# Sending token rows to expert slots: pacing each send by an earlier send's arrival instead of by a step's work

## The chip, the cores and the metric

The kernel runs on one core of a Trainium2 chip. A core has five engines that work side by side and wait for each other by semaphores: PE (TensorE, matrix products), DVE (VectorE), ACT (ScalarE), POOL (GpSimd) and SP (SyncE, which here only issues DMAs). DMAs run on 16 engines that all issuers share. The metric is the device time in microseconds; each figure is the median of several runs of the same program.

## The reference: what is computed

One transformer block over 8 sequences of 512 tokens of width 128. The rows are normalized. One branch is causal attention with 16 heads of width 8. The other is a mixture of experts: a shared feed-forward network for all tokens, and 8 expert networks of which each token uses the best two. Both read the same normalized rows, and their sum is added to the input.

```python
x = L0_attn_x
xn = _layernorm(x, axis=-1)
x = x + _L0_attn_ref(xn, ...) + _L0_ffn_ref(xn, ...)

# in _L0_ffn_ref
shared = _ffn(xf, shared_gate, shared_up, shared_down)
probs = jax.nn.softmax(xf @ gate_w.T, axis=-1)
topw, topi = jax.lax.top_k(probs, TOP_K)
...
acc + _ffn(xf, gw, uw, dw) * wcol[:, None]     # for each expert
```

with `_ffn` = `silu(x @ gw.T) * (x @ uw.T) @ dw.T`. There are 4096 tokens, hence 8192 pairs of a token and one of its experts.

## The kernel before

Attention runs in 160 steps: 32 groups of four heads (8 sequences with four groups each), five tiles of scores a group. A step fills a tile of scores on PE (`fill`, L322), takes its exponential on ACT (`weigh`, L446, line L450), and works seven tiles ahead on the rows' maxima (`look`, L810; PE L372, DVE L401 and L407). A step later the exponentials are multiplied with the values (`attend`, L464, line L473). From step 40 on (`BUSY`, L51) the causal mask of the diagonal tiles is no longer added by PE (L333) but cut out by POOL with a select (L458), queued behind the last send.

The feed-forward work is spread between the attention's steps, as a stream of pieces (`experts`, L718): 14 pieces of shared work (`EARLY`), then 36 pieces of routed work (two blocks of 128 slots each), then the rest of the shared work. A piece has three chunks (`chunk`, L663: four or eight products into gu, a tanh at L679, two DVE instructions at L680 and L681) and a product down (`down`, L694).

Routed work takes its rows from a table in HBM, `slots`, in which each expert has a run of blocks. `clear` (L871) first fills it with empty rows. `route` (L976), spread over the steps from the first one on, computes for each token its two experts and the two slots; the slots stand in SBUF (`slot`, L1055). Then each of the 32 rows of 128 tokens is sent twice, 64 indirect DMAs of 128 rows of 130 numbers (520 bytes), issued by POOL (`send`, L750, line L752). `load_slots` (L625) reads a block pair back into `s` after all 64 sends, the first three from POOL and the later ones from SP (L633), and `turn_slots` (L640) transposes it on PE (L648).

The order of PE, DVE, ACT and SP is the order in which the program writes their instructions. POOL's order is made by the tile framework from the dependencies and the program's order; every engine executes its own instructions in order, so one that waits holds up all behind it. In the sixth step (step 5) `route` puts the 64 sends on a list, and from then on each step takes two of them from it: one (L1248) gets a dependency on that step's exponential (`last_exp`), the other (L1259) on the last product of the step's gating (`last_gate`, L681), or on the exponential where the step has no gating. Two in a step make 32 steps, 5 to 36. Behind the sends POOL has the three loads of `s`, the selects from step 40 on, and later the returns of the routed results (L685).

Of the kernel before, what the change touches and what calls it, by code (L numbers as in the profile page):

```python
# [11 lines left out]
F32 = mybir.dt.float32  # L12
I32 = mybir.dt.int32
BF16 = mybir.dt.bfloat16
AF = mybir.ActivationFunctionType
ALU = mybir.AluOpType
# [7 lines left out]
SYNC = mybir.DependencyInfo(mybir.DependencyClass.Sync, mybir.DependencyReason.DATA)  # L24

P = 128
B, S, E = 8, 512, 128
H, D = 16, 8
NC = S // P
NT = B * NC  # L30
# [12 lines left out]
TOPK = 2  # L43
# [7 lines left out]
BUSY = 40  # L51
WIPED = 12
AT_ONCE = 2
EXPERTS_AT = 10
WEIGHTS_AT = 70
ROW = E + 2
# [9 lines left out]
def attn_moe_kernel(  # L66
# [15 lines left out]
    nc = tc.nc  # L82
    const = ctx.enter_context(tc.tile_pool(name="const", bufs=1))
# [45 lines left out]
    for i in range(NV):  # L129
        t = const.tile([P, NC, H, 32], F32, name=f"v_ext{i}")  # L130
# [65 lines left out]
    rows_attT = const.tile([P, NT, ROW], F32, name="rows_attT")  # L196
# [5 lines left out]
    for i in range(2 * TOPK):  # L202
        t = const.tile([P, NT], F32, name=f"best{i}")
        best.append(t)
    weight = const.tile([P, TOPK, NT], F32, name="weight")
    slot = const.tile([P, TOPK, NT], I32, name="slot")
# [3 lines left out]
    slots = dram1.tile([NB * BLK, ROW], F32, name="slots")  # L210
# [3 lines left out]
    def pool(name, bufs, **kw):  # L214
        return ctx.enter_context(tc.tile_pool(name=name, bufs=bufs, **kw))
# [3 lines left out]
    at = pool("at", 2)  # L219
# [102 lines left out]
    def fill(n, kind, j, bare):  # L322

        ps = w_ps.tile([P, 2, S], F32, name="scT")

        def part(out_, jj, width):
            q, k = rows_of(n, jj)
            i = NC - width // P
            nc.tensor.matmul(  # L329
                out_, lhsT=k[: QK + 3, ts(i, P)], rhs=q[: QK + 3, i * P :], start=True, stop=bare  # L330
            )
            if not bare:
                nc.tensor.matmul(out_[:, :P], lhsT=ident16, rhs=mask_k, start=False, stop=True)  # L333

        for t in range(2):
            if kind == "half":
                for u in range(2):
                    part(ps[:, t, ts(u, 2 * P)], 2 * t + u, 2 * P)
                continue
            at_ = 0  # L340
            for w in (S,) if kind == "wide" else (3 * P, P):
                part(ps[:, t, at_ : at_ + w], j + t, w)
                at_ += w
        return ps
# [96 lines left out]
                mT[ts(r, 16)],  # L441
            )

    last_exp, last_gate = [], []

    def weigh(n, kind, j, on_pool):  # L446

        ps = fill(n, kind, j, on_pool)
        pT = pr.tile([P, 2, S], F32, name="pT")
        last_exp[:] = [nc.scalar.activation(pT, ps, AF.Exp, scale=D**-0.5).ins]  # L450
        if on_pool:
            if kind == "half":
                diagonals = [pT.rearrange("p t (u k) -> p (t u) k", u=2)[:, :, :P]]
            else:
                diagonals = [pT[:, :, :P]] + ([pT[:, :, 3 * P :]] if kind == "mixed" else [])
            with tc.issue_after(sent[-1]):
                for d in diagonals:
                    nc.gpsimd.affine_select(  # L458
                        out=d, in_=d, pattern=[[0, d.shape[1]], [1, P]], compare_op=ALU.is_ge,
                        fill=0.0, base=0, channel_multiplier=-1,  # L460
                    )
        return pT
# [148 lines left out]
    later_pools = {}  # L611
    for_routed = ExitStack()
    sent, returned, stored = [], [], []

    def load_weights(k, c):

# [46 lines left out]
    def chunk(k, f):  # L663

        w, sT = turned[k]
        if f == 0:
            h_new = hid.tile([P, NF, PAIR], F32, name="h")
            hidden[k] = h_new
        h = hidden[k]
        gu = gu_ps.tile([P, 2, PAIR], F32, tag="gu", name="gu")  # L670
        for i in range(2):
            for c in range(len(w)):
                part = ts(c, PAIR // len(w))
                nc.tensor.matmul(  # L674
                    gu[:, i, part], lhsT=w[c][:, ds(i * FP + f * P, P)], rhs=sT[:, part],
                    start=True, stop=True,
                )
        th = res.tile([P, PAIR], F32, name="th")
        nc.scalar.activation(th, gu[:, 0], AF.Tanh, scale=0.5)  # L679
        nc.vector.scalar_tensor_tensor(th, th, 1.0, gu[:, 0], ALU.add, ALU.mult)  # L680
        last_gate[:] = [nc.vector.tensor_tensor(h[:, f], gu[:, 1], th, ALU.mult).ins]  # L681

    def give_back(k, c, o):

# [55 lines left out]
            load_weights(k + 2, 1)  # L740
        yield None, [partial(down, len(stream) - 1, c) for c in range(MB)]

    to_send = []

    def send_one(behind):

        if to_send:
            send(*to_send.pop(0), behind)

    def send(i, t, behind):  # L750

        d = nc.gpsimd.indirect_dma_start(  # L752
            slots, bass.IndirectOffsetOnAxis(ap=slot[:, i, t : t + 1], axis=0),
            rows_attT[:, t, :], None,
        )
        tc.add_manual_dep(d.ins, behind.name, SYNC, reason="in their step")
        if sent:
            tc.declare_no_dep(d.ins, group="sends", reason="no two pairs share a slot")
        tc.add_to_no_dep_group("sends", d.ins)
        sent.append(d.ins)  # L760
# [80 lines left out]
    def begin(step):  # L841
        for f in first.pop(step, []):
            more = f()
            if more is not None:
                more()
# [130 lines left out]
    def route():  # L976
# [73 lines left out]
        for i in range(TOPK):  # L1050
# [2 lines left out]
            own_sum = ro.tile([P, NT], F32, name=f"own_sum{i}")  # L1053
            nc.vector.tensor_reduce(own_sum, own, AX.X, ALU.add)
            nc.vector.tensor_copy(slot[:, i], own_sum)  # L1055
        to_send.extend((i, t) for t in range(NT) for i in range(TOPK))
        for _ in range(EXPERTS_AT):
            yield

# [93 lines left out]
    for b in range(5, B):  # L1153
        norm_rows(b)
    clear(0, AT_ONCE, unit_there)

# [25 lines left out]
    for t in range(FIRST):  # L1182
        step = t - FIRST
        begin(step)
        if t == NTILES:

            def onward():
                shift(0, parts_then)()
                clear(AT_ONCE, NB // WIPED, fetch(1))

# [32 lines left out]
    for n in range(B * NG):  # L1223
        b, g = divmod(n, NG)
        waiting = []
        for i, (kind, j) in enumerate(TILES):
            step = n * NTILES + i
            begin(step)
            if step in fetches:
                fetch(fetches[step])  # L1230
            on_pool = BUSY <= step < total_steps - 3
            waiting.append((kind, j, weigh(n, kind, j, on_pool)))

            if step - 1 in MORE:
                some_chunks(step, False)
                parts_then = look(step)
            else:
                parts_then = look(step)
                some_chunks(step, False)
            if step in light:  # L1240
                warm(5)
            parts_then()
            if step not in MORE and len(looked) < total_steps:
                prepare(*divmod(len(looked), NTILES))
            some_routing()
            if step >= WEIGHTS_AT:
                next(weighing, None)
            send_one(last_exp[0])  # L1248
            for f in late:
                f()  # L1250
            late = []
            if i == 1 and n % 2 == 0:
                av = av_ps.tile([P, S], F32, name="av")
            if i in (1, 3, 4):
                late = [partial(attend, n, waiting, av)]
                waiting = []
            side(step, 2)
            some_chunks(step, True)
            send_one((last_gate or last_exp)[0])  # L1259
            last_gate.clear()  # L1260
            if step in MORE:
                look(step)()
            if len(stored) == NB // MB:
                if not all_back:
                    for_routed.close()
                    later_pools["got"] = pool("got", 6)
                all_back.append(step)
            for _ in range(2 if len(all_back) > 1 else 0):
                if to_collect:
                    at_b = to_collect.pop(0)  # L1270
                    collect(at_b)
                    at_ = min(all_back[0] + 3 + 4 * at_b // 5, total_steps - 1)
                    due(at_, partial(weigh_second, at_b))
                    due(at_, partial(add_up, at_b, 0))
                    due(min(at_ + 1, total_steps - 1), partial(add_up, at_b, 1))

                    if (at_b + 1) * NC <= MB * EARLY and at_ + 2 < total_steps:
                        due(max(at_ + 2, last_shift), partial(store, at_b))
                    elif at_b < B - 1:
                        due(total_steps, partial(store, at_b))  # L1280
        if n == B * NG - 1:
            continue
        if n % 2:
            late.append(partial(evacuate, n, av))
            due(step + 2, partial(divide, n))
        if g == NG - 1:
            due(step + 3, partial(turn, b))
            due(step + 4, partial(join, b))
# [80 lines left out]
```

## Time and profile before

| | us |
|---|---|
| median of 3 runs (589.58 to 595.20) | 593.87 |
| the profiled execution's own time | 604.34 |
| its span | 602.6 |
| busy PE / DVE / ACT / POOL | 565.3 / 456.8 / 376.9 / 235.7 |
| sends on POOL: 64, first and last start | 67.6 and 187.3 |
| first PE instruction that reads `s` | 202.5 |

The profile shows one execution, with times from the start of its span. A group's line gives the source line, engine, operation, what is written and read, how often, and then the busy time, the mean of one in ns, the idle time of the engine just before these instructions and what ended most of it. A timeline's row gives start and length in us, and in brackets the idle time before it and its releaser. A send's length on POOL is the time of its issue; its bytes move later, and its arrival is told by a semaphore that gets sixteen steps.

### The profile page before, as it was taken

The numbers are of one execution on the slowest core, as the hardware profiler recorded it, in microseconds if no ns is written. First come the engines' busy times: TensorE is split into PE (matmuls) and PEld (weight loads), VectorE is DVE, ScalarE is ACT, GpSimd is POOL, SyncE is SP. The second block draws the span as 40 slices with busy tenths as digits, with TensorE's granted clock in tenths as the row PEclk, the third lists the DMA queues.
The fourth block names the chain that finished last, engine by engine and source line by source line (L and its number), as shares of the span: only waits on it lengthen the run. The fifth ranks groups of instructions, "written<-read, shape, count | busy, mean of one in ns | idle before, by whom it ended". The sixth has DMA issues, their size and how long they took to land.

```text
span 602.6 us, 13692 instructions
## 1 busy us (share of the span) xinstructions
PE 565.3 (94%) x4814; PEld 412.1 (68%) x4814; DVE 456.8 (76%) x1194; ACT 376.9 (63%) x698; POOL 235.7 (39%) x362
## 2 busy tenths in 40 slices
PE   6988899899988999999999999999999999999986
PEld 4756476567665677767777678777677777777643
DVE  6678958777765888777788687887687778787566
ACT  5624554564544767676667767686567767676574
POOL 9521345544554133334343334433434233433420
PEclk9888899999998999999999999999999999999987
DMA  7735244143144484839676585849666585843085
GB/s 215 240 71 225 77 127 112 41 124 90 45 112 129 131 230 133 250 101 265 208 175 206 168 226 177 207 156 217 194 198 212 173 211 198 218 136 109 4 265 154
DMA packets 52380, 98.39 MB, mean 163 GB/s; under 512 B 10070, under 2 KB 35546, under 8 KB 50152
## 3 DMA queue, kind: packets, MB, share of 16 engines
q1 hardware_dynamic: 45960, 83.65, 49.1%
q0 software_dynamic: 5360, 13.66, 6.7%
q8 instruction: 38, 0.62, 0.5%
q10 hardware_dynamic: 992, 0.21, 0.2%
q14 instruction: 30, 0.25, 0.1%
HBM read 73.36 MB, written 24.26 MB: 162 GB/s over the span
## 4 chain that ended last, share of the span: by engine, by line
PE 75%; ACT 9%; DVE 6%; DMA 4%; issue 3%; POOL 2%; SPq 1%; ACTq 0%; DVEq 0%; POOLq 0%
PE gu L674 21%; PE av L473 12%; PE y L701 11%; PE scT L329 10%; PE sc_diag L372 5%; PE sc_left L372 5%; ACT pT L450 2%; ACT sc_diag L360 2%; DMA qs<-dq 2%; DVE peaks L401 2%; PE qk_ps L246 2%; ACT th L679 1%; PE s_ps L648 1%; PE scT L333 1%; DMA w<-in_w_exp_dram 1%
## 5 line engine op out<-in xcount | busy, mean ns | idle before, releaser
L450 ACT ACTIVATE pT<-scT 128x1024 f32<-128x1024 f32 x160 | 164.0, 1025 | 66.6 <-PE scT L333 20.6
L685 POOL DMA_INDIRECT results<-o,goes x72 | 73.2, 1017 | 129.5 <-ACT o L707 118.6
L674 PE MATMUL gu<-sT,w 128*128 128x128 f32 x864 | 116.4, 277 | 1.7 <-DMA w<-in_w_exp_dram 1.1
L458 POOL TENSOR_SCALAR_AFFINE_SELECT pT<-pT 128x256 f32<-128x256 f32 (+1 forms) x163 | 70.3, 448 | 117.6 <-ACT pT L450 114.7
L401 DVE TENSOR_REDUCE peaks<-sc_diag 128x4 f32<-128x512 f32 x128 | 88.0, 687 | 33.5 <-PE sc_diag L372 22.5
L674 PEld LDWEIGHTS gu<-sT,w 128*128 128x128 f32 x864 | 108.1, 191 | 6.6 <-PE sc_diag L372 2.2
L329 PE MATMUL scT<-qs,ks 75*128 75x384 bf16 (+3 forms) x512 | 104.3, 304 | 5.1 <-ACT pT L450 5.0
L680 DVE SCALAR_TENSOR_TENSOR th<-th,gu 128x256 f32<-128x256 f32 x156 | 65.2, 418 | 38.5 <-ACT th L679 35.4
L679 ACT ACTIVATE th<-gu 128x256 f32<-128x256 f32 x156 | 59.7, 383 | 54.8 <-PE gu L674 31.5
L473 PE MATMUL av<-pT,v_ext 128*32 128x512 f32 (+3 forms) x1024 | 92.0, 455 | 0.0
L752 POOL DMA_INDIRECT slots<-rows_attT,slot x64 | 61.7, 964 | 76.1 <-ACT th L679 18.3
L372 PEld LDWEIGHTS <-qs 72*128 72x128 bf16 x896 | 65.1, 98 | 36.5 <-issue 18.0
L401 DVE TENSOR_REDUCE peaks<-sc_left 128x4 f32<-128x512 f32 x128 | 87.1, 680 | 0.0
L360 ACT CAST sc_diag<-mask_q 128x512 f32<-128x512 bf16 x115 | 68.1, 592 | 19.0 <-DVE peaks L401 10.0
L372 PE MATMUL sc_diag<-ks,qs 72*128 72x128 bf16 (+1 forms) x576 | 62.2, 225 | 8.9 <-ACT sc_diag L360 8.3
L681 DVE TENSOR_TENSOR h<-gu,th 128x256 f32<-128x256 f32 x156 | 66.2, 424 | 5.4
L701 PEld LDWEIGHTS y<-w,h 128*128 128x128 f32 x432 | 54.4, 191 | 22.3 <-issue 10.4
L701 PE MATMUL y<-w,h 128*128 128x128 f32 x432 | 64.1, 285 | 1.3 <-ACT v_ext L296 1.3
L372 PE MATMUL sc_left<-ks,qs 72*128 72x128 bf16 (+1 forms) x320 | 61.9, 275 | 3.3 <-DVE peaks L401 3.3
L329 PEld LDWEIGHTS <-ks 75*128 75x128 bf16 x512 | 47.0, 99 | 21.3 <-issue 10.2
L674 PE MATMUL gu<-xnT,ws_sb 128*128 128x256 f32 x192 | 53.0, 399 | 1.1 <-DVE h L681 0.9
L473 PEld LDWEIGHTS av<-pT,v_ext 128*32 128x32 f32 x1024 | 23.8, 110 | 31.1 <-issue 22.1
(185 smaller groups left out, 635.2 us busy)
## 6 DMA issues: line engine op xcount, KB each, us to landing
w<-in_w_exp_dram SPq DMA_DIRECT2D x72, 576.0 KB
qs<-dq SPq DMA_DIRECT2D x45, 192.0 KB
ks<-dk SPq DMA_DIRECT2D x45, 192.0 KB
slots<-empty POOLq DMA_DIRECT2D x6, 780.0 KB
s<-slots SPq DMA_DIRECT2D x33, 130.0 KB
r<-results SPq DMA_DIRECT2D x16, 256.0 KB
dq<-parts SPq DMA_DIRECT2D x7, 384.0 KB
dk<-parts SPq DMA_DIRECT2D x7, 384.0 KB
```

The lines of the kernel that those rows point to most:

```text
L329: nc.tensor.matmul(out_, lhsT=k[: QK + 3, ts(i, P)], rhs=q[: QK + 3, i * P :], start=True, stop=bare)
L360: nc.scalar.copy(diag_ps.rearrange("p (b k) -> p b k", k=P), mask_q.unsqueeze(1).to_broadcast([P, NC, P]),)
L372: nc.tensor.matmul(out_, lhsT=q[:QK, ts(c, P)], rhs=k[:QK, keys], start=start, stop=stop, skip_group_check=True,)
L401: nc.vector.tensor_reduce(peaks[:, i, 8 + 4 * t : 12 + 4 * t], banks[t].rearrange("p (b k) -> p b k", k=P), AX.X, ALU.max,)
L450: last_exp[:] = [nc.scalar.activation(pT, ps, AF.Exp, scale=D**-0.5).ins]
L458: nc.gpsimd.affine_select(out=d, in_=d, pattern=[[0, d.shape[1]], [1, P]], compare_op=ALU.is_ge, fill=0.0, base=0, channel_multiplier=-1,)
L473: nc.tensor.matmul(av[32 * jj : 32 * jj + 32, c * P :], lhsT=v_ext[b % NV][:, c, 4 * g + jj, :], rhs=weights, start=(n % 2 == 0 and c == 0 ...
L674: nc.tensor.matmul(gu[:, i, part], lhsT=w[c][:, ds(i * FP + f * P, P)], rhs=sT[:, part], start=True, stop=True,)
L679: nc.scalar.activation(th, gu[:, 0], AF.Tanh, scale=0.5)
L681: last_gate[:] = [nc.vector.tensor_tensor(h[:, f], gu[:, 1], th, ALU.mult).ins]
L685: d = nc.gpsimd.indirect_dma_start(results, bass.IndirectOffsetOnAxis(ap=goes_of[k][:, c : c + 1], axis=0), o, None, bounds_check=NP - 1, ...
L701: nc.tensor.matmul(y, lhsT=h[:, f, ts(c, P)], rhs=w[c % len(w)][:, ds(2 * FP + f * P, P)], start=(f == 0), stop=(f == NF - 1),)
```

## The change

The list of sends, the two calls in a step, and the notes of the last exponential and gating go. All 64 sends are written down at once where the list was made. From the third on, each has a memset of a scratch tile (128 x 384 numbers) on POOL ahead of it, and that memset waits for the arrival of the send two places in front; the send is queued behind its memset. The order of the sends stays the same.

```diff
+UNDER_WAY = 2
...
-    last_exp, last_gate = [], []
...
-        last_exp[:] = [nc.scalar.activation(pT, ps, AF.Exp, scale=D**-0.5).ins]
+        nc.scalar.activation(pT, ps, AF.Exp, scale=D**-0.5)
...
+    ticks = const.tile([P, 384], F32, name="ticks")
...
-        last_gate[:] = [nc.vector.tensor_tensor(h[:, f], gu[:, 1], th, ALU.mult).ins]
+        nc.vector.tensor_tensor(h[:, f], gu[:, 1], th, ALU.mult)
...
-    to_send = []
-
-    def send_one(behind):
-
-        if to_send:
-            send(*to_send.pop(0), behind)
-
-    def send(i, t, behind):
-
-        d = nc.gpsimd.indirect_dma_start(
-            slots, bass.IndirectOffsetOnAxis(ap=slot[:, i, t : t + 1], axis=0),
-            rows_attT[:, t, :], None,
-        )
-        tc.add_manual_dep(d.ins, behind.name, SYNC, reason="in their step")
+    def send(i, t):
+
+        with ExitStack() as order:
+            if len(sent) >= UNDER_WAY:
+                tick = nc.gpsimd.memset(ticks, 0.0)
+                tc.add_manual_dep(
+                    tick.ins, sent[-UNDER_WAY].name, SYNC, reason="few under way at a time"
+                )
+                order.enter_context(tc.issue_after(tick.ins))
+            d = nc.gpsimd.indirect_dma_start(
+                slots, bass.IndirectOffsetOnAxis(ap=slot[:, i, t : t + 1], axis=0),
+                rows_attT[:, t, :], None,
+            )
...
-        to_send.extend((i, t) for t in range(NT) for i in range(TOPK))
+        for t in range(NT):
+            for i in range(TOPK):
+                send(i, t)
...
-            send_one(last_exp[0])
...
-            send_one((last_gate or last_exp)[0])
-            last_gate.clear()
```

## The prediction

> **What bounds the kernel now.** I read the page first: busy time, then the chain of waits, then the costliest groups.
>
> ```profile
> PE 565.3 (94%) x4814; PEld 412.1 (68%) x4814; DVE 456.8 (76%) x1194; ACT 376.9 (63%) x698; POOL 235.7 (39%) x362
> PE 75%; ACT 9%; DVE 6%; DMA 4%; issue 3%; POOL 2%; SPq 1%; ACTq 0%; DVEq 0%; POOLq 0%
> L752 POOL DMA_INDIRECT slots<-rows_attT,slot x64 | 61.7, 964 | 76.1 <-ACT th L679 18.3
> ```
>
> PE is the bound and makes 75% of the chain; POOL has 2% of it. The third line is the 64 sends that the change re-orders: 0.964 us each on POOL. The releasers in front of them (view of waits, POOL, 67 to 205 us):
>
> ```profile
> POOL slots L752 <- ACT th L679: 18.3, 9, 2.5
> POOL slots L752 <- ACT pT L450: 14.3, 7, 3.7
> POOL slots L752 <- issue: 11.8, 30, 0.9
> POOL slots L752 <- DVE h L681: 7.6, 10, 2.0
> ```
>
> So POOL, not PE, waits for the steps: 61.7 us of sends and 58.8 us of idle time (76.1 less the 17.3 ahead of the first) make the stretch from 67.63 to 188.21 us. The question is therefore not what the sends cost but who waits for the last of them. The timeline of POOL at that place:
>
> ```profile
> 182.31 0.96 POOL L752 DMA_INDIRECT slots<-rows_attT,slot  x1 [0.31 <-DVE h L681]
> 183.58 0.96 POOL L752 DMA_INDIRECT slots<-rows_attT,slot  x1 [0.30 <-issue]
> 187.25 0.96 POOL L752 DMA_INDIRECT slots<-rows_attT,slot  x1 [2.71 <-DVE x_sb L711]
> 191.87 2.27 POOL L633 DMA_DIRECT2D s<-slots  x3 [3.66 <-DMA slots<-rows_attT,slot]
> 201.17 0.41 POOL L458 TENSOR_SCALAR_AFFINE_SELECT pT<-pT 128x256 f32<-128x256 f32 x1 [7.03 <-ACT pT L450]
> 204.55 0.41 POOL L458 TENSOR_SCALAR_AFFINE_SELECT pT<-pT 128x256 f32<-128x256 f32 x1 [2.97 <-ACT pT L450]
> ```
>
> The last send starts at 187.25 and lands at 191.1 by its semaphore. Three loads of s follow (free at 194.14), then POOL is idle for 7.03 us. The first s lands at 194.45, 2.6 us after its issue; PE reads it first at 202.5 (LDWEIGHTS s_ps). That is 8.0 us of slack for s, 7.0 us for the first select. Where the wire is busy (windows):
>
> ```profile
> 78.70:87.50 8.80, 8.52 (x79) 6.02 (x77) 5.79 (x12) 5.24 (x9) 4.06 (x5) 1.00 0.64 166
> 97.20:105.00 7.80, 7.20 (x67) 4.87 (x66) 6.19 (x15) 3.88 (x6) 4.51 (x5) 1.00 0.71 177
> 124.00:143.00 19.00, 18.37 (x161) 13.54 (x159) 14.75 (x35) 11.13 (x19) 9.40 (x10) 1.00 0.54 151
> 164.30:172.50 8.20, 7.36 (x61) 5.34 (x60) 6.15 (x15) 4.32 (x7) 4.47 (x6) 1.00 0.71 166
> 184.90:191.90 7.00, 5.30 (x29) 2.67 (x29) 3.35 (x8) 2.20 (x4) 0.99 (x2) 0.76 0.62 189
> ```
>
> The columns are length, busy PE, PEld, DVE, ACT, POOL, clock, DMA share, GB/s. Outside these five stretches the DMA share from 87 to 185 us is 0.12 to 0.19. In them q, k (or the first w) are moved by SP's queue, and a send lands late.
>
> **The change, part by part.**
>
> *Waits removed.* 60 waits of POOL for a step's exp or gating go. ACT and DVE did nothing for them, so nothing is saved there: 0.
>
> *Fills added.* 62 memsets of 128x384. POOL's memsets of 128x128 take 0.20 us and of 128x1560 1.39 us (groups by form), so 0.83 ns an element and 0.20 + 256 x 0.00083 = 0.41 us. 62 x 0.41 = 25.4 us of POOL, which had 58.8 us idle in this stretch.
>
> *Pitch where the wire is quiet.* In the trace a send lands (last of its sixteen semaphore steps) 2.27 us after its start: those started at 119.16, 121.15 and 125.67 took 2.27, 2.27 and 2.32. Send, fill, send: 0.96 + 0.41 + the 0.30 us that stand ahead of every send even when it waits for nothing ("issue" above) = 1.67 us. The send one place ahead started 1.67 us earlier, so at the next fill it is 1.67 + 0.96 = 2.63 us old and has landed. POOL, not the wait, sets the pace. Bounds: without the 0.30 us, 1.37 (then the wait sets (2.27 + 0.41 + 0.05)/2 = 1.37 as well). A select that follows a return mostly starts with no gap, but 12 of 72 show 0.25 to 0.27 us; if every fill pays that, 1.94. I take 1.67, as 41 of the 72 have no gap at all.
>
> *Pitch in the five bursts.* Sends started there landed after 6.5, 6.3, 5.0, 3.7 (first burst), 4.2, 6.2 (second), 6.2, 7.2, 4.3 (third), 5.0, 7.6, 3.5 (fourth), about 5.5 us; here the new wait binds. Two per 5.5 + 0.08 + 0.41 + 0.30 = 6.3 us is 3.1 us each. The bursts last 8.8 + 7.8 + 12 (from 131 to 143) + 8.2 + 5.5 = 42 us and hold 13.5 sends.
>
> *End of the stream.* Start 67.63, 1.3 for the second send, 42 in bursts, (62 - 13.5) x 1.67 = 81.0: the last send starts near 191.9 and lands at 194.2, 3 us later than before. s is issued then at 194.9 and lands at 197.5, 5.0 us before PE needs it. POOL is free at 197.2, 4 us before the exp of the first select ends. The cost is 0; what hides it is those 5 and 4 us. Without that cover each 0.1 us of pitch costs 6.3 us.
>
> *Rule against row.* The Trainium skill, "DMA: Bandwidth & Descriptors", section "Anatomy of one DMA — SWDGE (gpsimd) path", fits a DMA from this queue as 2.0 us plus bytes / 436e3. A send is 128 x 520 bytes, so an estimate of 2.15 us at all times. With it the wait never binds and the last send lands at 67.6 + 1.3 + 62 x 1.67 + 2.15 = 174.6. The quiet rows agree (2.27), the bursts (3.5 to 7.6) do not; I take the rows, 194.2. PE needs neither before 202.5.
>
> *Who queues behind a waiting fill.* On POOL: the other sends, the three s loads, the selects from step 40 on, later the returns. For them wait PE (s_ps, av) and, in SP's queue, the s loads from 208.27 on, which wait for all sends. Before step 40 nothing else is on POOL.
>
> *POOL's writes beside DVE.* No fill lies beside DVE work in the trace. The nearest row is the select: `second` (DVE, two operands in SBUF) has a median of 151 ns and up to 601, and the eight that meet a select average 0.25 us more. Small DVE instructions of that kind in the stretch: 7 each of L416, L421 to L424, 3 of L255, 4 of L261, 42. Fills cover 25.4 of 124 us; with the instruction's own length about a quarter are met: 42 x 0.25 x 0.25 = 2.6 us at most. The skill's "SBUF — State Buffer", section "SBUF: two separate sides", speaks against filling from GpSimd at all (it shares a port pair with VectorE, and one blocks the other for a whole instruction), but limits it for two-operand instructions to GpSimd work that reads SBUF; a memset only writes, so 0. Below nothing is excluded: a fill frees nobody. These instructions work some tiles ahead of their use and DVE is idle a quarter of the stretch; DVE has 6% of the chain, so 0.06 x 2.6, rounded to 0.2 us.
>
> *SP and the wire.* The same bytes move. At most two sends are under way instead of up to four in a burst, so q and k land sooner if anything. No PE, ACT or DVE wait from 60 to 215 us ends with a DMA: 0. PE's whole idle time in the five stretches is 0.3 + 0.6 + 0.6 + 0.8 + 1.7 = 4.0 us; that bounds a gain.
>
> *Sum.* 0 + 0 + 0.2 us, against the profiled execution's 604.34 us (602.6 of span and 1.7 around it). That run is 1.8% above the median of 593.87; a change of 0.2 us carries over as it is: 594.1 us.
>
> **Rivals.**
>
> *The stream comes late (slower).* If each fill pays the 0.27 us gap, the quiet pitch is 1.94: 67.6 + 1.3 + 42 + 48.5 x 1.94 = 205.0, landing 207.3, s there at 210.6, 8 us after PE asks for it. PE's order is fixed, so it stands: 602 us. If besides every send in a burst takes the worst 7.6 us (8.4 per two, 10 sends), 52 x 1.94 + 42 + 68.9 = 211.8, s at 217.5: +15 us, 609. It decides once the last send lands past 199.1 (202.5 - 2.6 - 0.8). For it: only 5 us of cover, 62 fills in one chain. Against: gapless starts are the common case.
>
> *Less crowding (faster).* If PE's idle time in the bursts comes from transfers, up to 4.0 us go: 590. Against it: no such wait in the view.
>
> *Fills hold DVE.* All 2.6 us on the path: 596.5.
>
> *The change doesn't pace by arrivals.* Outside the bursts the wait never binds and POOL's own 1.67 us sets the stream; the time is that of the likeliest case.
>
> **How the numbers follow.** Likeliest, nothing moves: 0.58, 594.1, own range 591 to 597. Late stream: 0.28, 597 to 609 around 602. DVE held: 0.07, 596.5. Less crowding: 0.07, 590, part of it below 588. About 1%, 5.9 us, is what a measurement of this kernel can tell from no change. Slower by more: most of the late case, 0.25. Faster by more: 0.05. Within: 0.70. The range leaves out the late case's upper part (0.11) and most of the gain (0.05): 589.5 to 604.
>
> **What would show it.** Right: fills of about 0.41 us, sends 1.7 us apart from 108 to 123 us and in pairs with gaps of several us behind DMA from 79 to 87 us; the last send lands between 185 and 199; PE's s_ps waits for no DMA; the span up to the first routed product (L674 with sT, 207.5 us) within 1 us. Wrong: PE waiting for s, or for a select of step 40, or POOL still in sends past 200 us; or DVE's small instructions grown beside the fills.

## The result, and the profile after

The changed kernel takes 614.87 us (median of 4 runs, 609.28 to 616.95). The kernel before, in the four runs beside it, takes 594.54 (589.58 to 595.94). The ratio is 1.0343, with a 95% interval of 1.0249 to 1.0437: 3.4% slower, above the top of the forecast range (604.0). The profiled execution took 616.26 us, with a span of 614.6.

The page's busy time, and two rows of its 40 slices of 15.4 us (busy share of PE and granted PE clock, in tenths):

```profile
span 614.6 us, 13755 instructions
PE 566.2 (92%) x4814; PEld 414.4 (67%) x4814; DVE 457.5 (74%) x1194; ACT 378.3 (62%) x698; POOL 262.0 (43%) x424
PE   6988899999995699999999998999999999999975
PEclk9888899999999699989999998999999999999999
```

PE runs the same 4814 products and is busy for nearly the same time as in the profile before (566.2 us against 565.3), so against that profile the added time is idle time. Most of it stands in one place: slices 13 and 14, from 184 to 215 us. The view of waits says for what (total, times, longest):

```profile
POOL ticks L747 <- DMA slots<-rows_attT,slot: 28.6, 18, 5.5
PE s_ps L648 <- DMA s<-slots: 11.4, 1, 11.4
PE gu L674 <- DMA w<-in_w_exp_dram: 4.4, 3, 2.9
```

PE waits once, for 11.4 us, for the first `s`. Before, no wait of PE there ended with a DMA. The timelines of POOL and of PE at that place:

```profile
194.66 0.97 POOL L752 DMA_INDIRECT slots<-rows_attT,slot  x1 [0.17 <-issue]
195.62 0.44 POOL L747 MEMSET ticks<- 128x384 f32 x1
196.24 0.96 POOL L752 DMA_INDIRECT slots<-rows_attT,slot  x1 [0.19 <-issue]
200.73 2.26 POOL L633 DMA_DIRECT2D s<-slots  x3 [3.52 <-DMA slots<-rows_attT,slot]
203.00 0.42 POOL L457 TENSOR_SCALAR_AFFINE_SELECT pT<-pT 128x256 f32<-128x256 f32 x1
```

```profile
192.61 0.94 PE L701 MATMUL y<-ws_sb,h 128*128 128x128 f32 x6
204.90 0.66 PE L648 MATMUL s_ps<-ident,s 128*128 128x128 f32 x2 [11.35 <-DMA s<-slots]
```

The last send starts at 196.24, and its sixteenth semaphore step comes at 200.2. Only then, at 200.73, are the loads of `s` issued. The first `s` is there at 204.9, but PE had come to it at 193.55. This is the sign that the prediction named for being wrong. The windows around it (length, busy PE, PEld, DVE, ACT, POOL, clock, DMA share, GB/s) show the second part of the cost:

```profile
185.00:192.00 7.00, 6.89 (x56) 4.50 (x54) 6.02 (x18) 6.23 (x10) 5.58 (x9) 1.00 0.13 40
192.00:204.00 12.00, 1.54 (x15) 0.90 (x14) 2.53 (x6) 1.90 (x4) 7.37 (x11) 0.74 0.74 234
204.00:218.00 14.00, 13.10 (x85) 10.59 (x86) 7.18 (x17) 6.61 (x13) 1.72 (x5) 0.74 0.58 144
```

The trace grants PE half its clock for 13.7 us, from 197.7 on: the clock falls 4.1 us after PE has stopped, and is still low for 6.4 us after it has gone on.

### The profile page after: what moved, and what is told of

It is laid out like the page before. It is cut to its first block, busy times and chain, and to the rows that moved or that the text cites. A ratio compares the mean times of both kernels' runs of the same rounds, so it can differ in the third digit from the quotient of the medians.

```text
span 614.6 us, 13755 instructions
## 1 busy us (share of the span) xinstructions
PE 566.2 (92%) x4814; PEld 414.4 (67%) x4814; DVE 457.5 (74%) x1194; ACT 378.3 (62%) x698; POOL 262.0 (43%) x424
## 5 line engine op out<-in xcount | busy, mean ns | idle before, releaser
L373 PEld LDWEIGHTS <-qs 72*128 72x128 bf16 x896 | 65.2, 98 | 32.1 <-issue 13.5
L752 POOL DMA_INDIRECT slots<-rows_attT,slot x64 | 62.4, 975 | 29.0 <-DVE slot L1054 16.4
L701 PE MATMUL y<-w,h 128*128 128x128 f32 x432 | 65.4, 288 | 1.3 <-ACT v_ext L297 1.3
```

Source lines behind the costliest of these rows:

```text
L373: nc.tensor.matmul(out_, lhsT=q[:QK, ts(c, P)], rhs=k[:QK, keys], start=start, stop=stop, skip_group_check=True,)
L701: nc.tensor.matmul(y, lhsT=h[:, f, ts(c, P)], rhs=w[c % len(w)][:, ds(2 * FP + f * P, P)], start=(f == 0), stop=(f == NF - 1),)
```

## The experiments

The kernel before was also run beside each group of experiments. It took 593.0 to 594.0 us there on three chips and 602.7 and 601.0 us on two others, so each run is compared with the runs of before on its own chip. Times "from the first exponential" count from the start of the first exponential of step 0 (40 to 43 us after the span's start).

**The kernel before, profiled again** (no edit).

> The kernel before, unchanged, for a second profile. Theory A (the stretch from 67 to 200 us was drawn out by some 9 us in the first profiled execution, and the sends, which ride on the steps, were drawn out with it): PE's first transpose of s at 192 to 195 us instead of 202.5, the last send at 176 to 181, the first s landed by 189, and an execution of 590 to 597 us. Rival (the steps really take that long in the kernel before, and the change made them faster): the transpose at 201 to 204 again, the execution near 604.

It took 592.23 us. POOL and PE:

```profile
177.10 0.96 POOL L752 DMA_INDIRECT slots<-rows_attT,slot  x1 [0.32 <-DVE x_sb L711]
182.96 2.26 POOL L633 DMA_DIRECT2D s<-slots  x3 [4.90 <-DMA slots<-rows_attT,slot]
```

```profile
191.01 0.38 PE L648 MATMUL s_ps<-ident,s 128*128 128x128 f32 x2
```

PE asks for `s` at 191.0, not at 202.5. The first `s` had landed at 186.8, 3.8 us after its issue, so the slack for it is 4.2 us here, not 8.0. The exponential of step 40 in this profile, in the changed kernel's and in the one from which the prediction was made:

```profile
188.46 1.02 ACT L450 ACTIVATE pT<-scT 128x1024 f32<-128x1024 f32 x1 [0.19 <-PE scT L329]
190.84 1.02 ACT L449 ACTIVATE pT<-scT 128x1024 f32<-128x1024 f32 x1 [0.19 <-PE scT L330]
200.06 1.02 ACT L450 ACTIVATE pT<-scT 128x1024 f32<-128x1024 f32 x1 [0.19 <-PE scT L329]
```

The first exponentials start at 40.09, 42.42 and 42.56. Counted from them, step 40 starts after 148.4 us here, 148.4 in the changed kernel, and 157.5 in the prediction's profile. The first profile's stretch was drawn out by 9 us, its sends with it, since each was tied to a step. A stream paced by arrivals does not move with the steps. Set against this second profile, whose steps agree with the changed kernel's to 0.1 us up to step 40, the changed kernel falls behind by 12.3 us at step 41, 14.3 at step 42, 17.3 at step 60, 22.0 at step 90 and 23.2 at the end.

**No waits, no fills.**

```diff
-UNDER_WAY = 2
+UNDER_WAY = 2 * 32
```

> The changed kernel with no fill and no wait at all: all sends in a row. Theory A (PE stands because the last send lands too late, and nothing else of the change costs): sends 1.27 us apart, the last at about 147 us and landed by 152, PE does not wait for s, and the time is that of the kernel before, 590 to 597 us. Rival B (the fills cost, by holding DVE): the same time, so this run does not tell B. Rival C (sends that no step paces crowd out the loads of q, k and the rows' maxima): PE waits inside 70 to 150 us and the time is 600 us or more.

It took 593.05 us (12 runs), ratio 0.9999 [0.9968, 1.0030]. The sends start 1.26 us apart, the loads of `s` are issued at 149.7 us, and PE waits for neither `s` nor a select. Sends that follow each other as fast as POOL issues them cost nothing here, and gain nothing: the rival of less crowding falls, and so does crowding as a cost.

**The wait alone, with a fill of one column.**

```diff
-                tick = nc.gpsimd.memset(ticks, 0.0)
+                tick = nc.gpsimd.memset(ticks[:, :1], 0.0)
```

> The changed kernel with its wait for the send two places in front, but a fill of one column (0.1 us) instead of 384. Theory A: quiet pitch 1.34 us, 14 sends in 42 us of bursts, last send at about 175 us, s landed by 181, no wait of PE, 590 to 597 us. Rival D (the wait of a send for an arrival is itself the cost, whatever the pitch): the time stays at 610 to 617 us.

It took 607.73 us, ratio 1.0264 [1.0198, 1.0331]. The last send was expected near 175 us; the loads of `s` are issued at 197.2:

```profile
POOL ticks L747 <- DMA slots<-rows_attT,slot: 33.4, 33, 3.8
PE s_ps L648 <- DMA s<-slots: 11.1, 1, 11.1
```

Without the fill's 0.43 us the waits come more often, 33 in place of 18. Where the wire is quiet two sends still take 3.06 us, 1.53 each, against 1.56 with the fill. A part of that is not the wait itself: behind a one-column fill that had waited, the send starts only 0.57 us later, and not 0.17 to 0.25 us as behind the long fill:

```profile
105.37 0.10 POOL L747 MEMSET ticks<- 128x1 f32 x1 [0.22 <-DMA slots<-rows_attT,slot]
106.04 0.95 POOL L752 DMA_INDIRECT slots<-rows_attT,slot  x1 [0.57 <-issue]
```

So the wait with what it brings along is enough for the late end, without the length of the fills.

**Four under way, fills kept.**

```diff
-UNDER_WAY = 2
+UNDER_WAY = 4
```

> The changed kernel with its fills of 384 columns, but four sends under way instead of two. Theory A: pitch 1.56 us nearly throughout, last send at about 168 us, no wait of PE for s, 590 to 597 us. Rival B (fills hold DVE, 62 of them as before): the time stays at 610 to 617 us although PE does not wait for s.

It took 593.23 us (20 runs), ratio 0.9988 [0.9966, 1.0011]:

```profile
POOL ticks L747 <- DMA slots<-rows_attT,slot: 6.9, 8, 2.0
```

The loads of `s` are issued at 174.5, and PE, at its transposes at 191.3, doesn't wait for them. 60 of the 62 fills are still there, and the time is that of before, so the fills don't cost time by holding DVE.

**PE kept at work during the stand.** 180 products more, whose result isn't used, ahead of the first routed transposes.

```diff
+KEEP = 180
...
+        if j == 0:
+            keep = gu_ps.tile([P, S], F32, tag="gu", name="keep_ps")
+            for _ in range(KEEP):
+                nc.tensor.matmul(keep[:, :P], lhsT=ident16, rhs=ident16, start=True, stop=True)
```

> The changed kernel with 180 more TensorE products (128x128 by 128 columns, bf16, into a spare PSUM tile) written ahead of the first routed transposes; their result is not used, and nothing that is computed is left out. TensorE then works for some 10 us (180 x 0.057 us) of the 11.4 us in which it stood waiting for s. Theory that the stand is followed by a halved clock (0.5 for 13.7 us after the change, 10.2 us with waits and no fills) and that this halving is a cost of its own: no halved clock behind s_ps, the stand's end unmoved, the steps after it 2 to 4 us earlier, the whole near 611 us. Rival, that the halved clock costs nothing because something else sets the pace behind the stand: the same time as the changed kernel, 613 to 616 us. If the added products push s_ps itself later than s lands, the time goes above that.

It took 616.36 us, on the chip where before takes 602.66: ratio 1.0202 [1.0130, 1.0275]. The products took 10.21 us, but the stream ended later on this chip (last send at 203.9), so PE stood for another 5.6 us, until 209.6. The trace shows half the clock for 6.8 us all the same, from 206.8 on, 4.0 of them behind the stand. What the halved clock costs by itself stays open by this run.

**The free stream, with `s` asked for late.** 118 fills between the last send and the loads of `s`. Beside it, the free stream with POOL's selects from step 29 on (the second edit).

```diff
-UNDER_WAY = 2
+UNDER_WAY = 2 * 32
+HOLD = 118
...
-        with tc.issue_after(sent[-1]):
+        with tc.issue_after(held_back[-1]):
...
+        with tc.issue_after(sent[-1]):
+            held_back.append(nc.gpsimd.memset(ticks, 0.0).ins)
+        for _ in range(HOLD - 1):
+            with tc.issue_after(held_back[-1]):
+                held_back.append(nc.gpsimd.memset(ticks, 0.0).ins)
```

> The free stream (no waits, no fills between the sends, which took 593.1 us) with 118 fills of 128x384 (0.43 us each, 50.7 us) between the last send and the loads of s; the mask selects of POOL stand behind them as they stand behind the last send. Only the time at which s is asked for is moved, to about 198 us, as after the change; the stream itself is as it was. Theory that the change costs what s comes late for TensorE (needed at 191 to 193 us, landing at 200 to 203): TensorE waits some 10 us for s, and the whole is 605 to 615 us, as after the change. Rival, that the waits of POOL inside the stream, or the pieces' crowding of the DMA engines, cost the time: about 594 us.

```diff
-BUSY = 40
+BUSY = 29
...
-UNDER_WAY = 2
+UNDER_WAY = 2 * 32
```

> The free stream (593.1 us), whose last send is at 147 us, and POOL cutting the causal mask from step 29 on instead of step 40, since it is free by then. TensorE is spared the mask products of 11 steps, some 3 a step of 0.056 us, about 2 us in all. Theory that TensorE bounds those steps: 591 to 592 us, 0.3% under the kernel before. Rival, that the select between exp and value product lengthens each such step's chain, or that POOL holds VectorE's port: 594 us or more.

They took 669.93 and 667.00 us, ratios 1.1094 [1.1019, 1.1168] and 1.1071 [1.1014, 1.1128], neither of them anything that was expected, where before takes 602.66. Windows of the first, and below of the free stream on the earlier chip:

```profile
90.00:110.00 20.00, 5.92 (x33) 3.42 (x32) 2.23 (x4) 1.76 (x3) 15.19 (x16) 0.50 0.16 53
110.00:130.00 20.00, 2.70 (x10) 1.95 (x8) 0.00 (x0) 1.02 (x1) 15.12 (x17) 0.50 0.16 53
130.00:147.00 17.00, 1.70 (x4) 0.42 (x4) 1.38 (x2) 0.00 (x0) 12.75 (x14) 0.50 0.16 51
```

```profile
90.00:110.00 20.00, 18.56 (x161) 13.15 (x161) 16.62 (x42) 9.49 (x15) 15.43 (x16) 1.00 0.41 115
110.00:130.00 20.00, 18.76 (x148) 12.86 (x147) 16.25 (x38) 13.23 (x24) 15.26 (x16) 1.00 0.35 110
130.00:147.00 17.00, 16.74 (x147) 11.89 (x145) 13.51 (x32) 8.34 (x13) 12.90 (x14) 1.00 0.43 119
```

POOL sends at the same rate in both. On this chip PE, DVE and ACT all but stop from 82 us until the sends end at 147 us, and PE is back at its full pace near 160. From 111 to 125 us PE's timeline shows one product at a time:

```profile
113.68 0.37 PE L703 MATMUL y<-ws_sb,h 128*128 128x128 f32 x1 [2.42 <-issue]
116.48 0.37 PE L703 MATMUL y<-ws_sb,h 128*128 128x128 f32 x1 [2.43 <-issue]
```

One product in 2.80 us, while the sends are 1.26 apart. So pacing the sends does protect something, on a chip of this kind: with two under way no such stop is seen on it. About a late `s` the run says nothing, since it was there long before the drawn-out steps needed it, and the other says nothing about earlier selects. The late `s` comes again below, with four under way.

**A longer fill.**

```diff
-    ticks = const.tile([P, 384], F32, name="ticks")
+    ticks = const.tile([P, 768], F32, name="ticks")
```

> The changed kernel with fills of 128x768 in place of 128x384 (about 0.8 us in place of 0.43). Theory that the end of the stream sets the time: quiet pitch about 1.9 us in place of 1.56, less than 62 x 0.37 = 23 us later since fills inside the waits of the bursts cost nothing: some 15 us, so the last send near 211 us, TensorE's wait for s some 26 us and the whole 627 to 635 us. Rival, that the arrivals pace the stream throughout and fills lie inside the waits: last send within 3 us of 196, the whole 613 to 619 us.

It took 622.46 us where before takes 602.66: ratio 1.0331 [1.0264, 1.0398].

```profile
POOL ticks L747 <- DMA slots<-rows_attT,slot: 25.5, 17, 3.3
PE s_ps L648 <- DMA s<-slots: 25.1, 1, 25.1
```

The fills are 62 x 0.32 = 20 us longer in all, and the last send is at 212.6, 8.7 us after that of the run with the 180 products on the same chip. So less than half of the fills' added time reaches the end of the stream; the rest lies inside waits that come anyway. The last send and the stand came near the expected 211 and 26 us all the same, and partly by luck: on this chip the stream with the shorter fills ended at 203.9, not at 196. The whole is below the expected 627 to 635. It exceeds the 611 to 615 us of the changed kernel on other chips by 8 to 11 us, somewhat less than the 11 to 14 us by which the stand has grown. The changed kernel as it is was not run on this chip.

**The changed kernel again, and four under way with `s` asked for late**, on a chip where before takes 592.98. In the second, only the end of the stream is held back, by 56 fills (`UNDER_WAY = 4`, `HOLD = 56`, otherwise the edit of the late free stream).

> The changed kernel as it is, once more, beside the runs below. Theory: last send 196 to 204 us after the span's start, TensorE at the first routed transposes (s_ps) at 191 to 194 us, a wait for s of 11 to 16 us, 613 to 617 us. The late wait for w (2.9 us at 372 us in the first profile) need not come back; if it does, it belongs to the change.

> The kernel with four sends under way, with 56 fills of 128x384 (0.43 us each, 24.1 us) between the last send and the loads of s, the mask selects of POOL behind them. Nothing in the stream is as in the change; s is asked for some 24 us later than with four under way, at 198 to 202 us. Theory that the lateness of s is what the change costs: TensorE waits 10 to 14 us for s, a halved clock behind it, 606 to 616 us. Rival, that the stream's own waits cost the time: 593 to 596 us, as with four under way.

> Four sends under way in place of two, fills kept, once more beside the kernel before. On the chip of its first runs it took 593.2 us against 593.9 before. On the chip of the second runs the kernel before took 602.7 us and a stream without waits stopped all engines for 76 us. Theory that four under way leave the engines room: last send near 172 to 180 us, no wait for s, 592 to 597 us on either chip, so under the kernel before where that takes 602. Rival, that four are enough to stop the engines where 64 are: a stop of tens of us between 80 and 170 us and 620 us or more there.

The changed kernel took 611.18 us, ratio 1.0307 [1.0247, 1.0367]; four under way 591.87, ratio 0.9987 [0.9953, 1.0020]; four under way with late loads 608.37, ratio 1.0236 [1.0179, 1.0293]. POOL and PE of the last:

```profile
199.60 2.26 POOL L635 DMA_DIRECT2D s<-slots  x3 [0.19 <-issue]
```

```profile
203.54 0.66 PE L650 MATMUL s_ps<-ident,s 128*128 128x128 f32 x2 [11.24 <-DMA s<-slots]
```

Its stream is that of the kernel with four under way, which costs nothing. Holding back what stands behind the stream adds 608.37 - 591.87 = 16.5 us, of which 11.2 are the stand itself. The 56 fills themselves are no rival, since 60 of them cost nothing above. This isolates the cause: it is not what happens in the stream, but when that which stands behind it can go. The wait for `w` of the first profile is absent from the changed kernel's second one (606.5 us), so it doesn't belong to the change in every execution; the other three runs, from 609.6 to 613.0, were not traced.

**The need for `s` moved, not the stream.** The changed kernel with the routed pieces from step 46.

```diff
-    first_step, routed_from, routed_to = -4, 42, 150
+    first_step, routed_from, routed_to = -4, 46, 150
```

> The changed kernel with the routed expert's pieces beginning at step 46 in place of 42 (four more of the early steps carry idle products in place of shared pieces, and the 108 steps' routed pieces are spread over 104). The stream of sends is left as it is; only the time at which TensorE asks for s is moved, from some 192 to some 207 us. Theory that the change costs what s comes late: no wait for s over 3 us, no halved clock behind it, and 6 to 14 us less than the changed kernel (600 to 608 us), although the added products and the denser steps cost some 2 us. Rival, that the time is lost inside the stream (fills, waits, crowding) or by the denser transfers behind it: within 3 us of the changed kernel, or above it.

Its runs spread from 606.5 to 623.2 us, too far for a comparison; the trace tells more. PE no longer waits for `s`, and stands all the same (PE's timeline, then POOL's):

```profile
206.45 1.94 PE L472 MATMUL av<-pT,v_ext 128*32 128x512 f32 x8 [10.98 <-POOL pT L457]
```

```profile
203.35 2.26 POOL L633 DMA_DIRECT2D s<-slots  x3 [6.52 <-DMA slots<-rows_attT,slot]
205.62 1.48 POOL L457 TENSOR_SCALAR_AFFINE_SELECT pT<-pT 128x256 f32<-128x256 f32 x4
```

Two things stand behind the end of the stream: the loads of `s`, and POOL's mask selects from step 40 on, with PE's value products behind them. With one out of the way, the other takes its place, for 11.0 us.

**Selects and routed pieces moved, together and apart**, and four under way, on the second chip on which before takes some 601 us. All three kernels with moved selects add the mask products of six steps on PE.

```diff
-BUSY = 40
+BUSY = 46
...
-    first_step, routed_from, routed_to = -4, 42, 150
+    first_step, routed_from, routed_to = -4, 46, 150
```

> The changed kernel with the routed pieces beginning at step 46 and POOL's mask selects beginning at step 46 as well, in place of 42 and 40; the stream of sends is as in the change. With the routed pieces alone moved, TensorE's value products waited 11.0 us for POOL's first select, which stood behind the last send and the loads of s. Theory that s and the selects are the two things that wait for the stream's end, and that nothing else of the change costs time: no wait of TensorE over 3 us between 188 and 215 us, no halved clock there, and a whole within 3 us of the next run's (four under way with the same two moves). Rival, that the paced stream costs time in itself: 8 us or more above the next run's.

> Four under way, with the routed pieces and POOL's selects beginning at step 46: what the two moves cost by themselves, with a stream that ends in time in either case. The early steps are cheaper (3.3 us by step 40 where the routed pieces alone were moved), 104 steps take the work of 108, 20 idle products and the mask products of six steps are added: 593 to 600 us.

> The changed kernel with POOL's mask selects beginning at step 46 in place of 40, all else as in the change. Theory that s and the selects both wait for the stream's end: TensorE still waits 11 to 14 us for s, and the whole stays within 3 us of the changed kernel (609 to 616 us). Rival, that the selects alone hold TensorE: 595 to 600 us.

> Four sends under way, fills kept, beside the kernel before on the chip of this call. Where the kernel before takes some 593 us: 591 to 596 us, no difference. Where it takes some 602 us, as on the chip on which a stream without waits stopped the engines: theory that four leave the engines room, 591 to 597 us, under the kernel before; rival, that four stop them too, 615 us or more.

With the selects alone moved the time is 613.56 us (610.01 to 620.03), ratio 1.0259 [1.0177, 1.0341], and PE waits 13.8 us for `s`: the selects alone don't explain the change either.

```profile
PE s_ps L648 <- DMA s<-slots: 13.8, 1, 13.8
```

Both moves together took 613.49 us with two under way and 611.33 with four, ratios 1.0204 [1.0141, 1.0268] and 1.0205 [1.0140, 1.0270]. That is within the 3 us expected, but it settles less than was hoped. The moves cost some 14 us by themselves (611.33 against 597.54 for four under way without them, where 593 to 600 had been expected with them), and two effects stand against each other: with four under way, steps 0 to 36 took 7.6 us longer than with two (138.5 against 130.9), while with two PE still stood 6.3 us for `s`, not the 3 at most that were expected. So the time didn't come back by moving the need, because moving it cost as much.

Four under way without the moves took 597.54 us, ratio 0.9946 [0.9918, 0.9974].

**Three under way, and before once more**, on a fifth chip.

```diff
-UNDER_WAY = 2
+UNDER_WAY = 3
```

> Three sends under way in place of two, fills kept. Two under way end the stream at 196 to 204 us and leave the engines alone; four end it at 172 to 175 us, but on the chip where the kernel before takes 601 us the steps up to 36 took 3.7 us longer with four than with two. Theory that the end of the stream needs only to come before 190 us: last send near 178 to 184 us, no wait for s over 1 us, 591 to 595 us where the kernel before takes 593, and 592 to 597 where it takes 601. Rival, that three already come too late in some executions: a wait for s of 2 us or more, 597 us or more.

> The kernel before, unchanged, for a profile on the chip of this call. Theory that the first profile of before (step 40 at 200 us, s_ps at 202.5 us, 845 recorded semaphore updates of TensorE) was that of a chip on which sends hold up the engines, and the second (191 us, 926 updates) that of one on which they don't: if the kernel before takes 600 us or more here, step 40 near 197 to 202 us and fewer than 880 updates; if 590 to 595 us, step 40 near 191 us and more than 900. Rival, that the drawn-out stretch comes and goes by chance on any chip: either of them with either time.

Three under way took 593.65 us (22 runs), ratio 1.0000 [0.9976, 1.0025]; its loads of `s` are issued at 183.0 and PE doesn't wait. Before, profiled, took 591.79, and its step 40 starts 146.7 us after the first exponential. So of three profiles of before, the first alone has the drawn-out stretch; the two on chips where before takes some 593 us have not.

## Why the prediction was wrong

**The step that failed: "PE reads it first at 202.5 ... That is 8.0 us of slack for s."** The need was read from one execution that took 604.34 us, 1.8% above the median, and the prediction said that "a change of 0.2 us carries over as it is". It doesn't. In that execution 9 us had been lost among the steps in front, and a stream tied to steps shifts with them. In an execution of the usual length PE asks for `s` 9 us earlier; a stream paced by arrivals ends no earlier. Whether the 9 us were chance or came from the chip stays open (last section). The prediction's 5.0 us of cover turned into 11.4 us of stand. Of these 16.4 us, 9.0 are the earlier need (202.5 less 193.55), and 7.4 the later `s` (204.9 less 197.5).

**The end of the stream was mis-sized, by 4.3 us at the last send (196.2 for 191.9).** The quiet pitch was better than taken, 1.56 us for 1.67 (0.96 + 0.43 + 0.17): over 62 sends that is nearly 7 us less. But the prediction's 13.5 sends at 3.1 us put some 19 us of waits into the bursts, and the view of waits shows 28.6. They are not longer than taken but more: 18 of 1.6 us on average, where two sends in 6.3 us make some 7 of 3 us. (The landings that the prediction lists for the bursts come from sends of which that trace holds only 2 to 13 of the sixteen steps, so they are lower bounds.) Three sends in a quiet place of the changed kernel's POOL, and its longest wait in a burst:

```profile
119.91 0.96 POOL L752 DMA_INDIRECT slots<-rows_attT,slot  x1 [0.16 <-issue]
120.87 0.43 POOL L747 MEMSET ticks<- 128x384 f32 x1
121.47 0.96 POOL L752 DMA_INDIRECT slots<-rows_attT,slot  x1 [0.17 <-issue]
...
134.02 0.96 POOL L752 DMA_INDIRECT slots<-rows_attT,slot  x1 [0.17 <-issue]
140.48 0.42 POOL L747 MEMSET ticks<- 128x384 f32 x1 [5.50 <-DMA slots<-rows_attT,slot]
```

The last send landed 3.9 us after its start where 2.3 had been taken, and the first `s` 4.2 us after its issue where 2.6 had been taken: both fell into the window from 192 to 204 us, in which 234 GB/s were moved. The 4.3 us of the last send, 1.6 more until it landed and 1.6 more for `s`, less 0.1 between the two, make the 7.4 us. The estimate of 2.15 us a send at all times, from the Trainium skill ("DMA: Bandwidth & Descriptors", section "Anatomy of one DMA — SWDGE (gpsimd) path"), would have had the stream landed at 174.6; the trace has 200.2. The prediction was right to follow the rows of its trace, which gave 194.2, and even they were short.

**"POOL, not the wait, sets the pace"** was right for the quiet places of the changed kernel. It does not mean that a shorter fill makes the stream faster: with the fill all but taken away the pace was nearly the same, 1.53 us.

**The rival of the late stream** named the mechanism, the place (PE's fixed order at the first routed transposes) and the sign. Its reason for the lateness did not come true: no quiet fill has the 0.27 us gap in front of it, and the waits in the bursts made the stream late. Its deciding point, a landing past 199.1 us, was passed by 1.1 us, which with the need at 202.5 would have been a stand of 2.4 us (204.9 less 202.5); the other 9.0 are the earlier need. That this rival came nearest to the 614.87 us is therefore in part luck.

**What was not in the sum.** A stand of PE was counted by its own length. From the first routed transposes to the second PE took 6.5 us, and 3.75 in the second profile of before; the low clock lies there, and step 42 is 14.3 us late after a stand of 11.4. In the changed kernel's second profile step 42 is 16.0 late after 13.9; in the late loads' profile steps 40 to 42 take 13.4 longer than with four under way, with a stand of 11.2. So 2.1 to 2.9 us more belong to each of these stands. PE's own rows hold them. Here are the windows from step 40 to step 42 in the changed kernel and in the second profile of before, and in each the four products into gu behind the transposes:

```profile
190.80:212.30 21.50, 10.15 (x60) 7.78 (x57) 6.91 (x18) 6.21 (x12) 8.81 (x14) 0.68 0.67 192
188.50:195.70 7.20, 6.90 (x60) 5.36 (x58) 6.63 (x19) 6.04 (x13) 0.81 (x2) 1.00 0.43 147
207.06 1.91 PE L674 MATMUL gu<-xnT,ws_sb 128*128 128x256 f32 x4
192.10 1.03 PE L674 MATMUL gu<-xnT,ws_sb 128*128 128x256 f32 x4
```

The same 60 products take 10.15 us in place of 6.90, 3.2 us longer, and the four into gu, with half the clock granted, nearly twice as long. In the changed kernel's second profile and in the late loads' the busy time grows by 2.1 us each, as much as the delay beyond the stand. So the traces put the rest of a stand's cost down to the halved clock; no run took the low clock away. After step 42 the first profile of the changed kernel loses some 9 us more, 2.9 of them at a place where the clock is granted at half for 3.4 us (262 us) and 4.7 where PE waits for `w` and the clock falls once more (372 us); the second profile loses nothing there. A loss of 6.3 us near 350 us, with a low clock, is also seen in the free stream (steps 86 to 90, against the second profile of before), whose median is that of before. What makes such a loss come or not stays open.

**What held.** The fills took 0.43 us for 0.41 and cost no time by DVE; the waits removed gave nothing in the undisturbed profiles; POOL's selects were late as well, hidden behind `s`, until the run that moved `s` brought them to light.

## What to carry to other kernels

Read the slack of a stream from the consumer's place in a run of the usual length, and count it on both sides: if the producer is tied to steps it moves with them, and if it is paced by itself it does not. A pace that is set by arrivals must be sized by the slow landings among other transfers (here up to 7.9 us, against 2.3 where the wire was quiet), and everything that stands behind the stream's end on the same queue (here two consumers) waits for it, so moving one shows the next. With two sends under way this stream ended 11 to 14 us too late, with three or four in time (three were run on one chip only). The smallest number that still ends in time with some us to spare suggests itself, since sends without a pause can hold up the other engines; whether three do better than four anywhere was not measured.

## What was not expected of the hardware

64 indirect sends issued without a pause by POOL, 1.26 us apart, were run on two chips. On one they cost nothing (593.05 us). On the other, in both kernels that had them, the other engines were held up, and the last step started 612.5 and 614.4 us after the first exponential, where it is 538.4 in the second profile of before. From 90 to 147 us the DMA view shows these queues, on the chip with the stop and on the other:

```profile
q0 software_dynamic: 1440, 3.00, 15.9%
```

```profile
q1 hardware_dynamic: 1888, 3.46, 22.0%
q0 software_dynamic: 1424, 3.00, 17.2%
q8 instruction: 4, 0.07, 0.4%
q14 instruction: 1, 0.01, 0.0%
```

On the first no packet of any other queue moved, not even of instructions; PE went on, for a part of the time at a product in 2.8 us. Whether the engines stopped because they were fed no instructions, or fetched none because they had stopped, these runs don't tell.

The chips fall into two kinds in all that was run. Where before takes 593 to 594 us, every trace holds 925 to 929 semaphore updates of PE; where it takes 601 to 603, every trace holds 821 to 874, though PE's program is nearly the same. The first profile of before, which took 604.34 us, holds 845, and agrees with the second kind: its lost 9 us may be a mild form of the same hold-up. That is a guess: before was not profiled again on a chip of the second kind. On the second kind, with two under way, step 40 came after 147 to 149 us, as on the first, and with four after 150.7. If the first profile is of this kind, pacing gives the engines back some us there, and the changed kernel then spends them, and more, on waiting for `s`. Four under way, with which `s` comes in time, is 0.5% faster than before on the one such chip where it ran, and equal to it on two of the others.
